# A graph-attention layer: the normalisation factor behind the row gather, a search moved from the loop into the drain, norms and transposes moved among TensorE's waits

## The chip, the cores and the metric

One core of a Trainium2 chip. The time is device microseconds of one execution, median of several; lower is better. A profile of one execution gives the spans and waits. The granted clock is the share of TensorE's full speed that the chip lets it run at; 1.00 is full speed. The core works with TensorE (PE), VectorE (DVE), ScalarE (ACT), GpSimd (POOL), SyncE (SP), and 16 DMA engines.

## The reference

```python
# x: 4096 x 512, adj: 4096 x 4096 (0, or up to 1e9), W: 512 x 2048, a: 4 heads x 1024
ht = (h @ W).reshape(N, 4, 512).transpose(1, 0, 2)
e = leaky_relu(src[:, :, None] + dst[:, None, :], 0.01) + adj[None]
att = softmax(e, axis=-1)
out = layernorm(x + einsum('hij,hjd->hid', att, ht).mean(axis=0))
```

The values of `adj` are so large that a row's softmax is nearly always 1 at its largest entry. The kernel therefore finds the largest entry of each row of `adj`, gathers that one row of `x`, multiplies it by the mean of the heads' weights, adds the row itself and normalises. A test (with norms as a bound) tells whether the second largest entry of any row comes near enough to matter; if so, a general path runs. It never runs on these inputs.

## The kernel before

4096 rows are 32 blocks of 128 (block 0 to 31). In step t of the loop VectorE reduces block t of `adj` to the maxima of 64 segments and finds the leading segment; GpSimd gathers that segment (`lead`, 64 numbers a row) from HBM; two steps later VectorE finds the place in it, and GpSimd gathers the row of `x` (`y`); a step later TensorE transposes it, ScalarE copies it out, TensorE multiplies it; ScalarE takes the statistics, and GpSimd makes of them the factor of normalisation (`rstd`). What follows the loop is called the drain. In the profile, MAX8 (`vector.max`) is the search for the eight largest entries of a row, and MATCH_VALUE_LOAD with FIND_INDEX8 (`max_index`) the search for their places.

```python
def find_segment(ib):
    seg = seg_of.pop(ib)
    nc.vector.max(out=top[:, ib, :], in_=seg)
    nc.vector.max_index(at, top[:, ib, :], seg)
    nc.gpsimd.tensor_tensor(row, at[:, 0:1], first[:, ib : ib + 1], op=OP.add)
    nc.gpsimd.indirect_dma_start(out=lead, in_=adj_segs, in_offset=...row...)
    ...
def find_inner(ib):
    nc.vector.max(out=inner[:, ib, :], in_=lead_of[ib])        # MAX8
def find_column(ib):
    find_inner(ib)
    nc.vector.max_index(within, inner[:, ib, :], lead_of.pop(ib))
    nc.gpsimd.tensor_tensor(col, at_of.pop(ib), within[:, 0:1], op=OP.add)
    gather_rows(ib, col)                                       # row gather: y
def finish_last(ib, residual):     # normalisation of one of the last four blocks, on VectorE
    ... tensor_add, bn_stats, bn_aggr ...
    nc.scalar.activation(r, mv[:, 1:2], AF.Sqrt, bias=eps)     # the root, on ScalarE
    nc.vector.reciprocal(r, r)
    nc.vector.tensor_scalar(hold[:, ib, :], o, mv[:, 0:1], r, ...)
# bound(0): largest norm, transposed by TensorE; bound(1): its root, broadcast by TensorE;
# bound(2): the bound itself on VectorE; test(): uses the bound, top and inner
# turn(ib): TensorE transposes y, ScalarE copies the result; products(ib, lo, hi): quarters lo to hi
```

In the profiles each engine takes its calls in program order: in the changed kernel ScalarE's copy for block 31 starts at 235.04 us, behind block 29's root at 234.84, and with the two calls swapped (a2_turn_first) at 230.71, ahead of the root at 234.13. So the place of a call among the others is its place in the engines' queues. All 32 stores are issued behind the loads (the last load at 200.92 us, the first store at 201.55); the last one, of block 31, waits for block 31's normalisation (its last part starts at 239.30, the store is issued at 240.14).

Of the kernel before, what the change touches and what calls it, by code (L numbers as in the profile page):

```python
# [9 lines left out]
F32 = mybir.dt.float32  # L10
# [9 lines left out]
P = 128  # L20
C = 512
E = 64
# [43 lines left out]
def leading_rows(ctx, tc, x, adj, W, a, out, ident, v, n_bad, any_bad):  # L66
# [7 lines left out]
    nc = tc.nc  # L74
    N, D = x.shape
    H = a.shape[0]
    KB, NB, S = D // P, N // P, N // E
    AHEAD = 5
    Q = 4
    PIECES = 4  # L80
    LATE = NB - Q
# [3 lines left out]
    small = ctx.enter_context(tc.tile_pool(name="small", bufs=5))  # L85
# [19 lines left out]
    def load_adj(ib):  # L105
        if 0 <= ib < NB:
            t = adj_t[ib] = adj_pool.tile([P, N], F32, name="adj_t")
            n = pieces(ib)
            for k in range(n):
                nc.sync.dma_start(t[:, ts(k, N // n)], adj_rows[ib][:, ts(k, N // n)])  # L110

    def load_x(lo, n):
        nc.sync.dma_start(hold[:, ds(lo, n), :], x_rows[:, ds(lo, n), :])
# [26 lines left out]
    top = once.tile([P, NB, 8], F32, name="top")  # L140
    inner = once.tile([P, NB, 8], F32, name="inner")
# [5 lines left out]
    seg_of, at_of, lead_of, y_t, yt_of, o_ps = {}, {}, {}, {}, {}, {}  # L147
# [12 lines left out]
# [3 lines that stand above are left out]
        at = small.tile([P, 8], U32, name="at")  # L163
        nc.vector.max_index(at, top[:, ib, :], seg)  # L164
        row = small.tile([P, 1], U32, name="row")
        nc.gpsimd.tensor_tensor(row, at[:, 0:1], first[:, ib : ib + 1], op=OP.add)  # L166
        lead = small.tile([P, E], F32, name="lead")
        nc.gpsimd.indirect_dma_start(  # L168
            out=lead, out_offset=None, in_=adj_segs,
            in_offset=bass.IndirectOffsetOnAxis(ap=row[:, :1], axis=0),  # L170
        )
        start = at_of[ib] = small.tile([P, 1], U32, name="start")
        nc.gpsimd.tensor_tensor(start, at[:, 0:1], width, op=OP.mult)  # L173
        lead_of[ib] = lead

    def gather_rows(ib, col):
        y = y_t[ib] = rows.tile([P, D], F32, name="y", bufs=4)
        nc.gpsimd.indirect_dma_start(  # L178
            out=y, out_offset=None, in_=x,
            in_offset=bass.IndirectOffsetOnAxis(ap=col[:, :1], axis=0),  # L180
        )

    def find_inner(ib):
        nc.vector.max(out=inner[:, ib, :], in_=lead_of[ib])

    def find_column(ib):
        find_inner(ib)
        within = small.tile([P, 8], U32, name="within")
        nc.vector.max_index(within, inner[:, ib, :], lead_of.pop(ib))  # L189
        col = small.tile([P, 1], U32, name="col")  # L190
        nc.gpsimd.tensor_tensor(col, at_of.pop(ib), within[:, 0:1], op=OP.add)  # L191
        gather_rows(ib, col)

    def find_column_in_row(ib):

        col = small.tile([P, 8], U32, name="col")
        nc.vector.max_index(col, top[:, ib, :], adj_t[ib])
        gather_rows(ib, col)

    def turn(ib):  # L200
        y = y_t.pop(ib)
        tp = psum.tile([P, KB, P], F32, name="tp", bufs=2)
        for kb in range(KB):
            nc.tensor.transpose(tp[:, kb, :], y[:, ts(kb, P)], ident)  # L204
        yt = yt_of[ib] = rows.tile([P, KB, P], F32, name="yt")
        nc.scalar.copy(yt, tp)  # L206
# [5 lines left out]
    def products(ib, lo=0, hi=KB):  # L212
        start = ib not in o_ps
        if start:
            o_ps[ib] = psum.tile([P, D], F32, name="o")
        for kb in range(lo, hi):
            nc.tensor.matmul(  # L217
                o_ps[ib], yt_of[ib][:, kb, :], w_sum[:, kb, :],
                start=(start and kb == 0), stop=(kb == KB - 1),
            )  # L220

    def row_norm(ib):
        sq = rows.tile([P, D], F32, name="sq")
        nc.scalar.activation(sq, hold[:, ib, :], AF.Square, accum_out=xx[:, ib : ib + 1])  # L224
# [8 lines left out]
    def rstd(i):  # L233
        nc.gpsimd.tensor_scalar(sd[:, i], sd[:, i], 1.0 / D, EPS, op0=OP.mult, op1=OP.add)  # L234
        nc.gpsimd.tensor_tensor(sd[:, i], sd[:, i], power[:, : i.stop - i.start], op=OP.pow)  # L235
        nc.gpsimd.tensor_mul(nm[:, i], nm[:, i], sd[:, i])  # L236
# [5 lines left out]
    def finish_last(ib, residual):  # L242

        o = o_ps.pop(ib)
        if residual:
            nc.vector.tensor_add(hold[:, ib, :], o, hold[:, ib, :])
            o = hold[:, ib, :]
        st = small.tile([P, nc.vector.BN_STATS_DIM], F32, name="st", bufs=2)
        nc.vector.bn_stats(st, o)
        mv = small.tile([P, nc.vector.BN_AGGR_DIM], F32, name="mv", bufs=2)  # L250
        nc.vector.bn_aggr(mv, st)
        r = small.tile([P, 1], F32, name="r", bufs=2)
        nc.scalar.activation(r, mv[:, 1:2], AF.Sqrt, bias=eps)
        nc.vector.reciprocal(r, r)
        nc.vector.tensor_scalar(hold[:, ib, :], o, mv[:, 0:1], r, op0=OP.subtract, op1=OP.mult)  # L255
# [52 lines left out]
    def bound(part):  # L308

        if part == 0:  # L310
            xm = once.tile([P, 1], F32, name="xm")
            nc.vector.tensor_reduce(xm, xx, axis=AX.X, op=OP.max)
            px = of_bound[0] = psum.tile([1, P], F32, name="px", bufs=1)
            nc.tensor.transpose(px, xm, ident)
        elif part == 1:
            nc.vector.tensor_reduce(xg, of_bound[0], axis=AX.X, op=OP.max)
            nc.scalar.activation(xg, xg, AF.Sqrt)
            pb = of_bound[1] = psum.tile([P, 1], F32, name="px", bufs=1)
            nc.tensor.matmul(pb, ones[0:1, :], xg, start=True, stop=True)
        else:  # L320
            nc.vector.tensor_mul(lead_by, of_bound[1], vn)
            nc.vector.tensor_scalar(lead_by, lead_by, 1.05, 110.0, op0=OP.mult, op1=OP.add)
# [3 lines left out]
    def test():  # L326
        a1 = top[:, :, 0]
        nc.vector.tensor_tensor(gap, top[:, :, 1], inner[:, :, 1], op=OP.max)
        size = once.tile([P, NB], F32, name="size")
        nc.vector.scalar_tensor_tensor(size, a1, -1.0, a1, op0=OP.mult, op1=OP.max)  # L330
        nc.vector.tensor_sub(gap, a1, gap)
        nc.vector.tensor_scalar(size, size, -(2.0 ** -22), lead_by, op0=OP.mult, op1=OP.subtract)
        nc.vector.scalar_tensor_tensor(gap, gap, 0.9999, size, op0=OP.mult, op1=OP.add)
        nc.vector.tensor_scalar(gap, gap, 0.0, None, op0=OP.is_gt)
# [18 lines left out]
    for t in range(NB):  # L353
        if t in x_at:
            load_x(*x_at[t])
        load_adj(t + AHEAD)
        middle = 1 if t == NB - 1 else 2
        segment_maxima(t, 0, middle)
        if t >= COLUMN:
            find_column(t - COLUMN)  # L360
        segment_maxima(t, middle, PIECES)
        find_segment(t)
        pair = t >= FINISH and t % 2 == 0
        if pair:
            rstd(slice(t - FINISH, t - FINISH + 2))
        if t < 2:
            mean_of_heads(t)
        elif t == 2:
            mean_of_heads(2)
            mean_of_heads(3)  # L370
        if t == 0:
            turn_a()
        turned = [(*vectors[0], turn_w(*vectors.pop(0))) for _ in range(vectors_at.get(t, 0))]
        if t == 16:
            head_norms()
        ib = t - PROJECT
        if ib >= 0:
            turn(ib)
            if ib < LATE:
                residual(ib)  # L380
        for some in turned:
            head_vector(*some)
        if ib >= 0:
            products(ib)
        if t >= STATS:
            stats(t - STATS)
            row_norm(t - STATS)
        if pair:
            finish(t - FINISH)
            finish(t - FINISH + 1)  # L390
# [4 lines left out]
    find_column(NB - 2)  # L395
    rstd(slice(NB - FINISH, NB - FINISH + 2))
    find_column_in_row(NB - 1)
    turn(NB - 3)
    products(NB - 3, 0, KB - 1)
    finish(NB - FINISH)  # L400
    finish(NB - FINISH + 1)
    for ib in range(LATE, NB):
        row_norm(ib)
    turn(NB - 2)
    products(NB - 3, KB - 1, KB)
    finish_last(NB - 4, True)
    find_inner(NB - 1)
    bound(0)
    products(NB - 2)
    bound(1)  # L410
    finish_last(NB - 3, True)
    bound(2)
    test()
    turn(NB - 1)
    for ib in (NB - FINISH, NB - FINISH + 1):
        store(nc.sync, ib, 1)
    residual(NB - 1)
# [244 lines left out]
```

## Time and profile before

| | before |
|---|---|
| time, median of the 4 runs beside the changed kernel | 248.11 us |
| span of the profiled run (247.19 us) | 245.3 us |
| busy: TensorE, VectorE, ScalarE, GpSimd | 82%, 77%, 45%, 40% |
| moved | 97.77 MB at 399 GB/s |
| end of the search through block 31's whole row (called F below) | 222.89 us |
| last store issued | 240.14 us |

A line of the order of time reads: start, duration, engine, line of the kernel, operation, output and input, shapes, how many were merged, and in brackets how long the engine had been idle and what released it. How the transfers and the drain look is shown in the prediction. Two more lines of VectorE, of block 30's tile, matter later:

```profile
204.71 2.27 DVE L155 TENSOR_REDUCE seg<-adj_t 128x32 f32<-128x2048 f32 x1
207.43 2.27 DVE L155 TENSOR_REDUCE seg<-adj_t 128x32 f32<-128x2048 f32 x1
```

Neither shows a wait. I read that as "the data had long been there". It had not: the packet records say that the last of the 16 engines delivered the first half at 204.66 and the second at 207.33, 0.05 and 0.10 us before VectorE took them.

### The profile page before, as it was taken

How to read it: one execution, taken by the hardware profiler on the slowest of the kernel's cores; microseconds unless marked ns; L12 is line 12 of the kernel's file. 1: busy time of each engine (PE TensorE's matmuls, PEld its weight loads, DVE VectorE, ACT ScalarE, POOL GpSimd, SP SyncE). 2: the span in 40 equal slices, each digit the busy share in tenths (PEclk: the TensorE clock that was granted, in tenths of full speed). 3: DMA queues.
4: the chain of work that ended last, by engine and by line, in shares of the span. 5: the costliest groups of instructions: out<-in, count | busy, mean ns of one | idle time of the engine just before them, and what ended most of it. 6: DMA issues, size and time to landing. Idle time of an engine off the chain costs nothing.

```text
span 245.3 us, 2538 instructions
## 1 busy us (share of the span) xinstructions
PE 200.4 (82%) x677; PEld 101.2 (41%) x678; DVE 188.7 (77%) x300; ACT 110.1 (45%) x266; POOL 97.6 (40%) x213
## 2 busy tenths in 40 slices
PE   0279948999999999999969777985969987987870
PEld 0135326555665555665334323332424432433320
DVE  2545686399689977998589979995998999966661
ACT  2012004044656565657645463744553846657110
POOL 1202423225616463646254535453455455652000
PEclk9999799599999999999999999999988999999995
DMA  7999999999999999999999999999999999999971
GB/s 257 435 428 414 422 423 425 418 424 408 425 416 415 415 414 422 422 402 431 418 418 413 426 412 421 408 424 416 416 414 390 412 408 400 409 401 376 402 294 55
DMA packets 16580, 97.77 MB, mean 399 GB/s; under 512 B 2472, under 2 KB 2472, under 8 KB 11184
## 3 DMA queue, kind: packets, MB, share of 16 engines
q1 hardware_dynamic: 12816, 87.82, 87.4%
q0 software_dynamic: 3584, 9.44, 10.0%
q10 hardware_dynamic: 160, 0.28, 0.3%
q8 instruction: 7, 0.11, 0.2%
q14 instruction: 13, 0.11, 0.1%
HBM read 89.15 MB, written 8.39 MB: 398 GB/s over the span
## 4 chain that ended last, share of the span: by engine, by line
DMA 35%; issue 26%; POOL 25%; DVE 7%; PE 4%; SPq 1%; POOLq 0%; ACT 0%; DVEq 0%
DMA adj_t<-in_adj_dram 29%; POOL y L178 8%; POOL lead L168 8%; DVE seg L155 5%; DMA lead<-in_adj_dram,row 3%; PE o L217 3%; DMA y<-in_x_dram,col 3%; POOL sd L235 3%; POOL row L166 2%; POOL start L173 2%; POOL col L191 1%; POOL sd L234 1%; POOL nm L236 1%; DVE hold L255 1%; SPq L110 1%
## 5 line engine op out<-in xcount | busy, mean ns | idle before, releaser
L155 DVE TENSOR_REDUCE seg<-adj_t 128x32 f32<-128x2048 f32 (+1 forms) x70 | 146.0, 2091 | 34.7 <-DMA adj_t<-in_adj_dram 34.5
L217 PE MATMUL o<-w_sum,yt 128*128 128x512 f32 x256 | 120.6, 613 | 1.3 <-ACT yt L206 1.3
L217 PEld LDWEIGHTS o<-w_sum,yt 128*128 128x128 f32 x256 | 47.1, 194 | 59.7 <-issue 47.0
L206 ACT COPY yt<-tp 128x512 f32<-128x512 f32 x32 | 18.8, 588 | 45.0 <-PE tp L204 44.9
L178 POOL DMA_INDIRECT y<-in_x_dram,col x32 | 32.2, 1008 | 16.7 <-POOL col L191 14.6
L168 POOL DMA_INDIRECT lead<-in_adj_dram,row x32 | 30.9, 964 | 15.5 <-POOL row L166 15.5
L204 PE MATMUL tp<-ident,y 128*128 128x128 f32 x128 | 19.7, 276 | 15.5 <-DMA y<-in_x_dram,col 15.3
L210 PE MATMUL o<-hold,ident 128*128 128x512 f32 x58 | 31.6, 627 | 0.8 <-DMA hold<-in_x_dram 0.8
L263 PE MATMUL o<-hold,ident 128*128 128x512 f32 x32 | 18.3, 724 | 15.7 <-DMA hold<-in_L_gnn_W_dram 15.7
L204 PEld LDWEIGHTS tp<-ident,y 128*128 128x128 f32 x128 | 14.4, 141 | 28.8 <-issue 27.4
L166 POOL TENSOR_TENSOR row<-at,first 128x1 uint32<-128x1 uint32 x32 | 5.9, 185 | 48.6 <-DVE at L164 47.4
L281 ACT COPY wt<-tp 128x512 f32<-128x512 f32 x16 | 9.2, 587 | 35.8 <-PE tp L279 35.8
L191 POOL TENSOR_TENSOR col<-start,within 128x1 uint32<-128x1 uint32 x31 | 5.9, 190 | 41.6 <-DVE within L189 41.6
L240 ACT ACTIVATE hold<-o,nm,sd 128x512 f32<-128x512 f32 x28 | 20.2, 771 | 2.5 <-POOL nm L236 2.5
L287 PEld LDWEIGHTS pv<-at_d,wt 128*128 128x128 f32 x128 | 17.2, 200 | 7.4 <-issue 3.9
L224 ACT ACTIVATE sq<-hold 128x512 f32<-128x512 f32 x32 | 19.8, 620 | 0.0
L231 ACT ACTIVATE sq<-o,nm 128x512 f32<-128x512 f32 x28 | 19.3, 688 | 0.9
L263 PEld LDWEIGHTS o<-hold,ident 128*128 128x128 f32 x32 | 7.2, 236 | 24.2 <-POOL row L166 10.4
L229 ACT ACTIVATE sq<-o 128x512 f32<-128x512 f32 x28 | 17.0, 607 | 0.0
L264 ACT ACTIVATE w_sum<-o 128x512 f32<-128x512 f32 x4 | 2.4, 598 | 31.7 <-PE o L263 31.7
L287 PE MATMUL pv<-at_d,wt 128*128 128x2 f32 x128 | 16.0, 249 | 0.6 <-ACT wt L281 0.6
L279 PEld LDWEIGHTS tp<-ident,hold 128*128 128x128 f32 x64 | 7.9, 142 | 6.9 <-issue 6.9
(73 smaller groups left out, 116.7 us busy)
## 6 DMA issues: line engine op xcount, KB each, us to landing
adj_t<-in_adj_dram SPq DMA_DIRECT2D x27, 2048.0 KB
out_dram<-hold SPq DMA_DIRECT2D x31, 256.0 KB
hold<-in_x_dram SPq DMA_DIRECT2D x7, 1024.0 KB
adj_t<-in_adj_dram SPq DMA_DIRECT2D x12, 512.0 KB
hold<-in_L_gnn_W_dram SPq DMA_DIRECT2D x4, 1024.0 KB
adj_t<-in_adj_dram SPq DMA_DIRECT2D x4, 1024.0 KB
hold<-in_x_dram SPq DMA_DIRECT2D x4, 256.0 KB
lead<-in_adj_dram,row POOLq DMA_INDIRECT x32, 5.8
```

The source lines that it names most:

```text
L155: nc.vector.tensor_reduce(seg_of[ib][:, ts(k, S // n)], adj_t[ib][:, ts(k, N // n)].rearrange("p (s e) -> p s e", e=E), axis=AX.X, op=OP.max,)
L168: nc.gpsimd.indirect_dma_start(out=lead, out_offset=None, in_=adj_segs, in_offset=bass.IndirectOffsetOnAxis(ap=row[:, :1], axis=0),)
L178: nc.gpsimd.indirect_dma_start(out=y, out_offset=None, in_=x, in_offset=bass.IndirectOffsetOnAxis(ap=col[:, :1], axis=0),)
L204: nc.tensor.transpose(tp[:, kb, :], y[:, ts(kb, P)], ident)
L206: nc.scalar.copy(yt, tp)
L210: nc.tensor.matmul(o_ps[ib], ident, hold[:, ib, :], start=True, stop=False)
L217: nc.tensor.matmul(o_ps[ib], yt_of[ib][:, kb, :], w_sum[:, kb, :], start=(start and kb == 0), stop=(kb == KB - 1),)
L224: nc.scalar.activation(sq, hold[:, ib, :], AF.Square, accum_out=xx[:, ib : ib + 1])
L231: nc.scalar.activation(sq, o, AF.Square, bias=nm[:, i], accum_out=sd[:, i])
L240: nc.scalar.activation(hold[:, ib, :], o_ps.pop(ib), AF.Identity, bias=nm[:, i], scale=sd[:, i])
L263: nc.tensor.matmul(o, ident, hold[:, w_at + kb * H + h, :], start=(h == 0), stop=(h == H - 1))
L287: nc.tensor.matmul(pv[:, kb, h : 2 * H : H], wt[:, k, :], at_d[:, k, h : 2 * H : H], start=(k == 0), stop=(k == KB - 1),)
```

## The change

Its intent: get VectorE through the last blocks sooner by taking a MAX8 out of each (the search can use `top`, which holds the same largest value; the second largest in the segment is needed only by the test at the end), let the row gather go ahead of the factor on GpSimd, and fill TensorE's waits in the drain.

```diff
-        lead = small.tile([P, E], F32, name="lead")
+        lead = small.tile([P, E], F32, name="lead", bufs=2 * Q + 1)
...
     def find_column(ib):
-        find_inner(ib)
+        if ib < LATE - Q:                     # LATE - Q is 24
+            find_inner(ib)
-        nc.vector.max_index(within, inner[:, ib, :], lead_of.pop(ib))
+        nc.vector.max_index(within, top[:, ib, :], lead_of[ib])
...
-        find_segment(t)
         pair = t >= FINISH and t % 2 == 0
         if pair:
             rstd(slice(t - FINISH, t - FINISH + 2))
+        find_segment(t)
...                                            # the drain
     find_column_in_row(NB - 1)
+    for ib in range(LATE, NB):
+        row_norm(ib)
     turn(NB - 3)
+    bound(0)
     products(NB - 3, 0, KB - 1)
     finish(NB - FINISH)
     finish(NB - FINISH + 1)
-    for ib in range(LATE, NB):
-        row_norm(ib)
     turn(NB - 2)
     products(NB - 3, KB - 1, KB)
+    bound(1)
+    bound(2)
     finish_last(NB - 4, True)
-    find_inner(NB - 1)
-    bound(0)
-    products(NB - 2)
-    bound(1)
+    for ib in range(LATE - Q, NB):
+        find_inner(ib)
+    test()
+    products(NB - 2, 0, KB - 1)
     finish_last(NB - 3, True)
-    bound(2)
-    test()
     turn(NB - 1)
+    products(NB - 2, KB - 1, KB)
```

## The prediction

> **What bounds the kernel now.** I read the page first, then stretches of the last 45 us, then the chain of waits, then the order of time on VectorE and GpSimd before the drain. The page's slices of 6.13 us say that the transfers set the pace almost to the end:

> ```profile
> DMA  7999999999999999999999999999999999999971
> GB/s 257 435 428 414 422 423 425 418 424 408 425 416 415 415 414 422 422 402 431 418 418 413 426 412 421 408 424 416 416 414 390 412 408 400 409 401 376 402 294 55
> ```

> Both rows are flat through slice 38. 97.77 MB go through; at the 415 GB/s of the middle that alone is 236 us of the 245.3 us span. Nothing in the change removes a byte, so only the last two slices are open to it. The stretches of 2 us show where the full load ends:

> ```profile
> 234.00:236.00 2.00, 2.00 (x6) 0.80 (x5) 1.53 (x5) 0.29 (x1) 0.00 (x0) 1.00 1.05 402
> 236.00:238.00 2.00, 1.79 (x6) 0.38 (x4) 1.07 (x5) 0.00 (x0) 0.00 (x0) 1.00 0.74 283
> 238.00:240.00 2.00, 0.00 (x0) 0.00 (x0) 1.57 (x4) 0.29 (x1) 0.00 (x0) 1.00 0.08 25
> 240.00:242.00 2.00, 0.00 (x0) 0.00 (x0) 0.11 (x1) 0.00 (x0) 0.00 (x0) 0.54 0.36 131
> ```

> The last two columns are DMA share and GB/s. Output stores fill the engines until about 237.5; then they stand idle until the last store, issued at 240.14, of row block 31. So the arithmetic that leads to the last store trails the transfers by some 2.6 us, and that is all a shorter drain can win: even a perfect one leaves about 245.8 of 248.46 us. The chain of waits over the drain (start, us, what):

> ```profile
> 219.21 6.63 DMA y<-in_x_dram,col
> ...
> 228.74 3.44 PE o L217 x8
> 232.17 0.31 PE px L319 x2
> 232.48 0.59 PE tp L204 x4
> 233.07 0.86 PE o L210 x2
> 233.93 2.66 PE o L217 x6
> 236.58 0.15 PE px L338 x2
> 236.73 1.07 PE o L217 x2
> ...
> 239.30 0.81 DVE hold L255
> ```

> A row gather of 6.63 us, then TensorE nearly back to back, then the last normalisation on VectorE. Ahead of it, one row block on VectorE:

> ```profile
> 201.33 0.22 DVE L184 MAX8 inner<-lead 128x8 f32<-128x64 f32 x1
> 201.65 0.09 DVE L189 MATCH_VALUE_LOAD within<-inner,lead 128x8 f32 x1
> 201.73 0.22 DVE L189 FIND_INDEX8 within<-inner,lead 128x8 uint32<-128x64 f32 x1
> 201.86 2.27 DVE L155 TENSOR_REDUCE seg<-adj_t 128x32 f32<-128x2048 f32 x1
> ```

> From 188.7 to 215.9 VectorE never waits for a transfer: it trails the matrix, block after block, in steps of 5.56 us. The MAX8 takes the place of 0.32 us (201.33 to 201.65): 0.22 busy, 0.10 until the search that reads its result. And GpSimd puts the normalisation factor (L234 to L236) between two gathers:

> ```profile
> 212.40 0.19 POOL L234 TENSOR_SCALAR sd<-sd 128x2 f32<-128x2 f32 x1
> 212.68 0.72 POOL L235 TENSOR_TENSOR sd<-sd,power 128x2 f32<-128x2 f32 x1
> 213.48 0.20 POOL L236 TENSOR_TENSOR nm<-nm,sd 128x2 f32<-128x2 f32 x1
> 213.63 0.19 POOL L191 TENSOR_TENSOR col<-start,within 128x1 uint32<-128x1 uint32 x1
> ```

> The index search for that column (`within`) was over at 212.01, so 1.6 us of the gather's delay is the factor.

> [...] here the instruction shows 0.96 us and the chain 6.63 us, so I count gathers from issue to landing.[...]

> **The change, part by part.** The order of instructions was compared with the one before.

> 1. *MAX8 of `lead` leaves the loop for blocks 24 to 31.* The search uses `top`, whose first entry is the same value. Six leave the loop; the one in block 26's step is swallowed by the 0.83 us wait for data at 187.05. Five are worth 5 x 0.32 = 1.6 us: the loop on VectorE ends at about 214.3 instead of 215.9. Packets counted up in the trace put the last piece of the matrix at 211.7, where VectorE begins it at 214.2 now and would at 212.6: late enough.

> 2. *Factor before the segment's row, after the row gather* (on even steps). Block 29's row gather, issued at 214.21, loses both the 1.6 us of factor ahead of it and most of VectorE's 1.6: some 2.4 us earlier. In return block 30's segment gather, issued at 211.14, is now behind the factor (0.19 + 0.72 + 0.20 and gaps, 1.2 us): from a VectorE shift of 1.3 it keeps about 1.2, so 209.9. It landed 5.8 us after issue by the packets (211.14 to 216.95), so 215.7 now, and VectorE, ready at 214.3, waits 1.4 us for it, as it waits 1.42 us now.

> 3. *Search of block 30's column and of block 31's full row.* From landing to the end of the search in 64 elements it is 218.40 - 216.95 = 1.45 now; without the MAX8 in between about 0.95. With 4.5 us for the search through 4096 (4.42 and its value load) the searches end at F = 220.5 instead of 222.89: 2.35 us earlier. Both last row gathers go that much earlier.

> 4. *The drain after F.* Norms (four squares of 0.62 us) come ahead of a copy on ScalarE, and end at about 220.3, just under F. On TensorE the bound's transposition waits for F (+0.5), three quarters of block 29's products follow (2.84), the transposition of block 30 (F + 3.2, its row then being there), the last quarter, and the bound's broadcast at F + 4.6. VectorE stands idle from F + 0.8 until then; now it does block 28's normalisation in that time. After the broadcast VectorE has, in order: bound 0.7, block 28's normalisation 2.65 (228.98 to 231.63 for the same five now), eight MAX8 at about 0.14 apart and one latency 1.3, test 0.95, and 1.65 of block 29 until its root. That root stands on ScalarE ahead of the copy that the last products need. Root 0.3, copy to first product 0.64, products, count and last quarter 4.07 (233.76 to 237.83), last statistics to store 2.31 (237.83 to 240.14). Sum: F + 4.6 + 0.7 + 2.65 + 1.3 + 0.95 + 1.65 + 0.3 + 0.64 + 4.07 + 2.31 = F + 19.2.

> Now it is 240.14 - 222.89 = F + 17.25. So the drain starts 2.35 us earlier and is 1.9 us longer, and the store goes out at 239.7 instead of 240.14. I predict a gain of about 0.5 us: 248.0 us.

> **Rivals.** (a) *TensorE sets the drain's end*: if VectorE does its share faster, products for block 31 would follow those of block 30 without a pause, at about F + 11, and the store go out 2.5 to 3 us earlier: 245.8, the transfers' floor above. For it: TensorE's own work does shrink in pauses, as intended. Against: the root of block 29 is issued ahead of the last copy. (b) *No head start*: if block 30's segment gather lands no earlier, because its 5.8 us stretch under load or the factor holds it, F stays at 222.3 or so and the longer drain shows: store at 241.5, 249.8 us.[...] (c) *The transfers decide*: stores now run at full load until 237.5 whatever VectorE does; then a store at 238 or 240 costs only itself. It caps (a), and makes the loop's part worth nothing by itself.

> **Range and chances.** Runs of before spread over 1.26 us, some 0.5% of the time. With the shift of F unsure by 1 us and VectorE's stretch by 1, I take 246.2 to 249.4. Two per cent is 5 us: faster by that would need bytes saved (0.03); slower by that needs a wait nobody planned (0.02).

> **What would show it.** Right: no MAX8 in VectorE's last six steps and eight together near 230; the loop's last segment search ending about 214.3; block 31's full-row search ending about 220.5; VectorE idle some 4 us behind it, until the bound's broadcast; TensorE idle before the last block's products, released by ScalarE's copy, and that by the root; the transfers' full load ending at 237.5 still. Wrong: TensorE without that pause and a store before 238 (rival a), or a full-row search that ends after 222 (rival b). If the slices in the middle gain or lose GB/s, everything here is beside the point.

## The result, and the profile after

The changed kernel took 250.77 us in the median (250.05 to 250.99, 4 runs), the kernel before 248.11 (247.33 to 249.02, 4 runs). Ratio 1.0101, 95% interval 1.0058 to 1.0144: slower by about 1%, clearly not a gain, and outside the stated range. A ratio here is the mean time of one kernel's runs over that of the other's of the same rounds, so not quite the ratio of the medians. Executions over 1.5% slower than the fastest of the same kernel are left out of the means.

The page's transfers, in 40 slices (now of 6.22 us):

```profile
DMA  7999999999999999999999999999999999999921
GB/s 253 413 424 420 424 428 419 415 425 405 421 419 414 420 406 431 416 412 425 411 422 416 418 420 420 405 422 416 414 408 399 410 405 399 409 395 395 391 94 54
```

The middle is as before: no bytes were won or lost. Slice 39 fell from 294 to 94 GB/s: the stores were done, and the core waited longer for its last one. It was issued at 243.76 instead of 240.14, 3.62 us later. That splits into two parts.

**The loop did not get shorter.** VectorE at block 30, in order of time:

```profile
205.55 2.29 DVE L155 TENSOR_REDUCE seg<-adj_t 128x32 f32<-128x2048 f32 x1 [1.18 <-DMA adj_t<-in_adj_dram]
207.75 0.08 DVE L191 MATCH_VALUE_LOAD within<-top,lead 128x8 f32 x1
207.82 0.22 DVE L191 FIND_INDEX8 within<-top,lead 128x8 uint32<-128x64 f32 x1
208.40 2.29 DVE L155 TENSOR_REDUCE seg<-adj_t 128x32 f32<-128x2048 f32 x1 [0.36 <-DMA adj_t<-in_adj_dram]
```

The MAX8 is gone from between the reductions, as planned. But VectorE now waits 1.18 and 0.36 us for the two halves of the tile: 1.54 us, the 1.6 us that the five MAX8 were to save. The last reduction of the loop ends at 216.03 (before: 215.38), block 30's segment gather is issued at 212.13 (before: 211.14), and F is 223.52 instead of 222.89: 0.63 us later, not 2.35 earlier. Of these, 0.44 us were there already at the first reduction of block 27, which waits for its data in both kernels and starts at 188.32 instead of 187.88.

**The drain got longer**, from F + 17.25 to F + 20.24. Its chain in order of time:

```profile
228.15 0.16 DVE L323 TENSOR_TENSOR lead_by<-px,vn 128x1 f32<-128x1 f32 x1 [3.90 <-PE px L321]
...
231.06 1.10 DVE L184 MAX8 inner<-lead 128x8 f32<-128x64 f32 x8
...
234.84 0.29 ACT L255 ACTIVATE r<-mv,eps 128x1 f32<-128x1 f32 x1 [4.47 <-DVE mv L253]
235.04 0.57 ACT L208 COPY yt<-tp 128x512 f32<-128x512 f32 x1
...
235.66 4.54 PE L219 MATMUL o<-w_sum,yt 128*128 128x512 f32 x6 [2.62 <-ACT yt L208]
```

VectorE stands idle for 3.90 us until the bound is broadcast, then does block 28's normalisation, eight MAX8, the test and the start of block 29's normalisation, before the root (L255) can go. Only behind that root stands the copy that block 31's products need, and TensorE has waited 2.62 us for it. All of this was foreseen. What was not is the 4.54 us. The same six pieces in the kernel before:

```profile
233.76 2.82 PE L217 MATMUL o<-w_sum,yt 128*128 128x512 f32 x6
```

The stretches of 2 us (length, then busy time with count of TensorE, its weight loads, VectorE, ScalarE, GpSimd, then TensorE's granted clock, DMA share, GB/s) say why:

```profile
232.00:234.00 2.00, 1.04 (x3) 0.19 (x1) 1.86 (x10) 0.00 (x0) 0.00 (x0) 1.00 1.05 404
234.00:236.00 2.00, 0.34 (x1) 0.34 (x2) 1.57 (x5) 0.77 (x2) 0.00 (x0) 0.95 1.04 399
236.00:238.00 2.00, 2.00 (x3) 0.73 (x3) 1.55 (x4) 0.29 (x1) 0.00 (x0) 0.50 0.55 209
238.00:240.00 2.00, 2.00 (x4) 0.58 (x2) 0.55 (x1) 0.00 (x0) 0.00 (x0) 0.70 0.30 112
```

After the pause the granted clock is 0.50. The clock records have it at half from 235.81 for 3.413 us, beginning right as the products start (235.66). Before, it was 1.00 from 185.53 to 240.14. In both profiles the clock changes only at whole multiples of 3.413 us from one another: this fall comes 75.1 us after the end of the one before (160.71), 22 times 3.413. Such a stretch of 3.413 us, counted from the changes of the same profile, is called a window below. In the window before this fall, from 232.39, TensorE had 0.80 us of products; the last section comes back to that.

### The profile page after: what moved, and what is told of

The parts are those of the page before. It is cut to its first block, busy times and chain, and to the rows that moved or that the text cites.

```text
span 248.9 us, 2520 instructions
## 1 busy us (share of the span) xinstructions
PE 203.3 (82%) x677; PEld 102.4 (41%) x678; DVE 186.3 (75%) x300; ACT 109.4 (44%) x266; POOL 97.3 (39%) x213
## 2 busy tenths in 40 slices
DMA packets 16581, 97.77 MB, mean 393 GB/s; under 512 B 2473, under 2 KB 2473, under 8 KB 11185
## 4 chain that ended last, share of the span: by engine, by line
DMA 44%; PE 23%; issue 10%; DVE 10%; POOL 8%; ACT 2%; SPq 0%; POOLq 0%; DVEq 0%
DMA adj_t<-in_adj_dram 20%; DMA hold<-in_x_dram 13%; PE o L219 12%; DMA hold<-in_L_gnn_W_dram 11%; DVE seg L155 4%; PE o L265 3%; PE pv L289 3%; POOL lead L168 2%; POOL y L178 2%; PE o L212 2%; DVE col L199 2%; PE tp L281 1%; PE tp L206 1%; POOL sd L237 1%; DVE st L251 1%
## 5 line engine op out<-in xcount | busy, mean ns | idle before, releaser
L155 DVE TENSOR_REDUCE seg<-adj_t 128x32 f32<-128x2048 f32 (+1 forms) x70 | 146.2, 2094 | 41.2 <-DMA adj_t<-in_adj_dram 40.7
L178 POOL DMA_INDIRECT y<-in_x_dram,col x32 | 30.8, 963 | 17.8 <-POOL col L193 15.7
L168 POOL DMA_INDIRECT lead<-in_adj_dram,row x32 | 32.2, 1007 | 13.9 <-POOL row L166 13.9
L265 PE MATMUL o<-hold,ident 128*128 128x512 f32 x32 | 22.1, 856 | 16.3 <-DMA hold<-in_L_gnn_W_dram 16.3
L212 PE MATMUL o<-hold,ident 128*128 128x512 f32 x58 | 31.4, 624 | 0.0
L233 ACT ACTIVATE sq<-o,nm 128x512 f32<-128x512 f32 x28 | 19.2, 687 | 0.9
L265 PEld LDWEIGHTS o<-hold,ident 128*128 128x128 f32 x32 | 8.4, 275 | 27.1 <-POOL row L166 11.7
L289 PEld LDWEIGHTS pv<-at_d,wt 128*128 128x128 f32 x128 | 16.3, 191 | 6.8 <-ACT wt L283 3.7
L289 PE MATMUL pv<-at_d,wt 128*128 128x2 f32 x128 | 15.3, 244 | 0.6 <-ACT wt L283 0.6
```

Source lines behind the costliest of these rows:

```text
L155: nc.vector.tensor_reduce(seg_of[ib][:, ts(k, S // n)], adj_t[ib][:, ts(k, N // n)].rearrange("p (s e) -> p s e", e=E), axis=AX.X, op=OP.max,)
L168: nc.gpsimd.indirect_dma_start(out=lead, out_offset=None, in_=adj_segs, in_offset=bass.IndirectOffsetOnAxis(ap=row[:, :1], axis=0),)
L178: nc.gpsimd.indirect_dma_start(out=y, out_offset=None, in_=x, in_offset=bass.IndirectOffsetOnAxis(ap=col[:, :1], axis=0),)
L212: nc.tensor.matmul(o_ps[ib], ident, hold[:, ib, :], start=True, stop=False)
L233: nc.scalar.activation(sq, o, AF.Square, bias=nm[:, i], accum_out=sd[:, i])
L265: nc.tensor.matmul(o, ident, hold[:, w_at + kb * H + h, :], start=(h == 0), stop=(h == H - 1))
```

## The experiments

Theory 1: the loop's moves are worth nothing, because the transfers hold VectorE; the drain loses by its order (root before copy, more work in VectorE's chain) and by the pauses, with TensorE's clock at half behind them (0.50 for 3.413 us in the profile above). Rivals: the clock is by the way; the moves in the loop lose, not the drain; VectorE's chain or late gathers set the end whatever the order. Each kernel ran beside the kernel before on the same chip. All gave correct results.

| run | median us | before | ratio (95%) | F | last store | F to store |
|---|---|---|---|---|---|---|
| kernel before, first profile | 248.11 | | | 222.89 | 240.14 | 17.25 |
| changed, first profile | 250.77 | 248.11 | 1.0101 (1.0058 to 1.0144) | 223.52 | 243.76 | 20.24 |
| a8_changed_again | 250.69 | 247.51 | 1.0151 (1.0103 to 1.0199) | 223.06 | 243.28 | 20.22 |
| a1_fill | 249.16 | 247.52 | 1.0065 (1.0018 to 1.0112) | 222.99 | 241.56 | 18.57 |
| a9_two_fills | 249.10 | 247.78 | 1.0046 (1.0024 to 1.0068) | 223.69 | 242.22 | 18.53 |
| a2_turn_first | 247.86 | 247.52 | 1.0004 (0.9967 to 1.0042) | 222.82 | 240.45 | 17.63 |
| a3_drain_only | 248.13 | 247.52 | 1.0028 (0.9981 to 1.0075) | 222.56 | 240.66 | 18.10 |
| a4_factor_only | 247.46 | 247.51 | 1.0017 (0.9976 to 1.0057) | 222.85 | 239.93 | 17.08 |
| a5_defer_only | 246.76 | 247.51 | 0.9980 (0.9938 to 1.0022) | 222.53 | 241.66 | 19.13 |
| a6_reordered | 247.19 | 247.52 | 0.9977 (0.9930 to 1.0024) | 223.03 | 239.99 | 16.96 |
| a7_old_loop_new_drain | 246.77 | 247.51 | 0.9967 (0.9933 to 1.0001) | 222.93 | 239.67 | 16.74 |
| a10_mended_filled | 246.03 | 247.78 | 0.9938 (0.9914 to 0.9962) | 222.95 | 238.84 | 15.89 |

F and the last store are of the profiled execution, one per kernel; the times are of six executions, in the first two rows of four.

### a1_fill: work for TensorE in the second pause

```diff
+    idle = psum.tile([P, D], F32, name="o")
+    for _ in range(3):
+        nc.tensor.matmul(idle, ident, hold[:, NB - 1, :], start=True, stop=True)
     residual(NB - 1)
```

> The changed kernel with three products of the identity (their sum thrown away) put into TensorE's pause of 2.62 us before block 31's products. Theory 1 (the pause halves TensorE's granted clock, and that costs 1.7 us after it): the clock stays at 1.0 in the drain, the six halves of products take 2.84 us instead of 4.54, the last store goes out 1.7 us earlier, about 249.1 us. Theory 2 (the products are slow for another reason, such as loads on the memory or missing records): products still near 4.5 us, 250.8 us. If the extra products themselves delay block 31's residual by more than the pause, the start of its products moves past the copy.

The clock stayed at 1.0 in the drain, and the six pieces of product, still behind the same root and copy, were back to their length:

```profile
235.16 2.84 PE L219 MATMUL o<-w_sum,yt 128*128 128x512 f32 x6
```

F to last store fell by 1.67 us, the median came out at 249.16 against the expected 249.1. In the profile three products that nobody reads bring the drain's products back to full speed: theory 1's clock is shown, its rival is out. In time this run alone isn't clear of the changed kernel's first comparison (the intervals 1.0018 to 1.0112 and 1.0058 to 1.0144 overlap); a9_two_fills against a8_changed_again is.

### a2_turn_first: the copy before the root

```diff
     products(NB - 2, 0, KB - 1)
-    finish_last(NB - 3, True)
     turn(NB - 1)
+    finish_last(NB - 3, True)
```

> The changed kernel with block 31's transposition and copy put before block 29's normalisation in the program, so ScalarE copies before it takes the root. Theory 1 (the order of the root and the copy on ScalarE makes TensorE wait, and the pause halves the clock): TensorE without the pause, copy right behind the transposition (about 231.3), then VectorE's chain of three normalisations is the end: last store about 2.5 us earlier than 243.76, 248.3 us. Rival (VectorE's chain sets the end anyhow, the copy is only in its shadow): less than 1 us gained, 250 us or more.

ScalarE copied right behind the transposition, TensorE had no pause there (block 31's products start at 232.17; the two before them start at 231.32 and take 1.02 us), and the last store came 3.3 us earlier than in the changed kernel's first profile (2.6 of it between F and the store). The end is now VectorE's chain, three normalisations one behind the other:

```profile
230.71 0.59 ACT L208 COPY yt<-tp 128x512 f32<-128x512 f32 x1 [1.04 <-PE tp L206]
...
238.15 0.68 DVE L251 BATCH_NORM_STATS2 st<-o 128x6 f32<-128x512 f32 x1
```

The last statistics start as soon as VectorE is through with what stands before them, 2 us after the products. The swap of two lines undoes nearly all of the loss: 1.0004.

### a3_drain_only: the old loop with the changed drain

```diff
         (in words: the loop as in the kernel before; the drain as in the changed kernel, but)
-    for ib in range(LATE - Q, NB):
-        find_inner(ib)
+    find_inner(NB - 1)
```

> The kernel before in its loop (factor and MAX8 where they were), the changed drain (with one MAX8 instead of eight in it). Theory 1 (the drain's order is the loss, the loop's two moves are worth nothing because the transfers hold VectorE): as slow as the changed kernel less seven MAX8 at 0.14 us, about 249.8 us. Rival (the loop's moves are what loses, the drain gains as intended): 247.5 us or less.

248.13 us: slower by 0.3%, with an interval that includes no change, and not by the expected 0.9%. The expectation took half the clock for granted. With one MAX8 in the chain instead of eight the root came earlier, TensorE's pause was 1.74 us instead of 2.62, and the clock did not fall in it (the six pieces behind it took 2.84 us). 249.8 less the 1.7 us of clock is 248.1. So the drain's order without the seven extra MAX8 costs little (F to last store 0.85 us longer than before); most of the rest comes with the pause and the half clock after it.

### a8_changed_again: the changed kernel once more

> The changed kernel itself, once more and beside the next three. Theory 1: the drain's last products again behind a TensorE pause of about 2.6 us; whether the clock halves there depends on where the pause falls, so the single times may split by up to 1.7 us. Median 249.5 to 250.8 us, ratio about 1.008. If it comes out within 0.3% of the kernel before, the loss of the first comparison was chance.

1.0151: the loss is no chance. The profile has a turn that I had not expected. The second pause (2.62 us) was there again, at full clock: the products after it took 2.84 us. Instead the clock had fallen at the first pause, where TensorE waited for block 28's row:

```profile
212.00:214.00 2.00, 1.36 (x4) 0.29 (x2) 2.00 (x5) 0.95 (x2) 1.69 (x4) 1.00 1.04 411
214.00:216.00 2.00, 0.00 (x0) 0.00 (x0) 1.91 (x3) 0.00 (x0) 0.45 (x1) 0.89 0.98 390
216.00:218.00 2.00, 1.27 (x5) 0.90 (x6) 0.30 (x2) 0.82 (x2) 1.06 (x2) 0.50 1.07 409
218.00:220.00 2.00, 2.00 (x3) 0.96 (x4) 1.70 (x4) 1.97 (x7) 1.07 (x4) 0.50 1.04 408
220.00:222.00 2.00, 2.00 (x3) 0.68 (x3) 2.00 (x1) 2.00 (x7) 1.47 (x4) 0.50 1.05 403
```

Half clock from 215.58 for two windows (6.827 us). Block 28's products took 5.96 us instead of 3.70, which pushed block 29's transposition to 223.62 (220.84 in the first profile) and with it the broadcast (5.9 us behind F instead of 4.2). F to last store is 20.22 us by this way and 20.24 by the other. A pause of 2.62 us before block 31's products was followed by half clock in one run and by full clock in the other. Where it lay differed. In the first profile it fell into one window whole (232.39 to 235.81), and TensorE had 0.80 us of products in that window; here the edge of two windows (236.06) cut it, and the first of them, from 232.65, had 1.62 us of products (see the last section).

### a9_two_fills: work in both pauses

```diff
+        if t == NB - 1:
+            busy = psum.tile([P, D], F32, name="o")
+            for _ in range(2):
+                nc.tensor.matmul(busy, ident, w_sum[:, 0, :], start=True, stop=True)
         if ib >= 0:
             turn(ib)
... and the three products of a1_fill
```

> The changed kernel with idle products in both of TensorE's pauses: two ahead of block 28's transposition, three ahead of block 31's products. Theory 1[...]: the clock stays at 1.0 from 185 us to the end of the products, searches to last store F + 18.6, median 248.6 to 249.0 us, against 250.7 for the changed kernel. What is left over the kernel before, some 1.2 us, is then the drain's order (root before copy, eight MAX8 in the chain). Rival (the clock is by the way): 250 us or more, as the changed kernel.

The clock was at 1.0 from 185.62 to 243.64, and block 28's eight products took 3.70 us (5.96 in a8_changed_again). F to last store was 18.53 (expected 18.6), median 249.10 (0.1 us over what was expected), and the six times lie within 1.4 us (a1_fill's, with one pause filled, within 3.2). The interval is clear of a8_changed_again's. What is left, 0.5%, goes with the drain's order and its eight MAX8: F to last store is 1.28 us longer than before.

### a4_factor_only: only the factor moved

```diff
-        find_segment(t)
         pair = ...
         if pair:
             rstd(slice(t - FINISH, t - FINISH + 2))
+        find_segment(t)
```

> The kernel before with the factor alone moved ahead of the segment's search. Theory A[...]: block 27's row gather issued at about 202.2 instead of 203.09, the second half of block 30's tile complete at about 208 instead of 207.3, VectorE waits for it, the searches end no earlier than in the kernel before (222.9, within 0.4): 247.5 to 248.2 us. Rival (taking the factor out of the gather's way is a gain): block 30's and 31's row gathers earlier by 1 us, 246.8 us.

Time and F are about as theory A has them (247.46, 222.85), but not in the way it expected: block 27's gather did not move (203.05), and VectorE shows no wait for block 30's tile (it starts on the second half 0.10 us after its last part, 207.77 after 207.67). Block 29's gather did go out 1.0 us earlier (213.19 instead of 214.21), the way the prediction said (it had 2.4 us from both moves), and it is worth nothing: block 30's and 31's gathers (219.16, 223.61), which the end hangs on, stand where they stood.

### a5_defer_only: only the MAX8 deferred

```diff
         (lead with 9 buffers, search on top, MAX8 in the loop only below block 24, as in the change)
     find_column_in_row(NB - 1)
+    for ib in range(LATE - Q, NB - 1):
+        find_inner(ib)
     turn(NB - 3)
```

> The kernel before with the MAX8 of blocks 24 to 30 alone deferred into VectorE's idle 1.3 us behind the full-row search. Theory A (the transfers hold VectorE's loop, so time taken off VectorE turns into waiting for the next tile): new waits of 1 to 1.6 us in all for block 30's and 31's tiles, loop end no more than 0.4 us earlier than 215.4: 247.3 to 247.9 us. The prediction's step (five MAX8 at 0.32 us bring the loop's end and all behind it 1.6 us forward): loop end at 213.8, 246.2 us.

The direct test of the prediction's first step. VectorE at block 30:

```profile
205.29 2.29 DVE L155 TENSOR_REDUCE seg<-adj_t 128x32 f32<-128x2048 f32 x1 [1.21 <-DMA adj_t<-in_adj_dram]
```

The saved time is waited away at this tile; the loop's last reduction ends at 215.42, against 215.38 before and 213.8 by the prediction. The 0.36 us by which F is earlier comes from the MAX8 no longer standing between block 30's segment and its search. The median, 246.76, is lower than theory A said, though its interval includes no change at all. The six times are 246.4 to 246.8 four times, and 248.6 and 248.8. The profiled one is a slow one of these: clock at half for 3.4 us from 218.74, after a pause of 2.55 us before block 28's transposition; block 28's eight products took 5.40 us instead of 3.70. That the other slow one has the same cause is likely, but no profile shows it.

### a6_reordered and a7_old_loop_new_drain: the drain mended

```diff
     finish(NB - FINISH + 1)
+    finish_last(NB - 4, True)
     turn(NB - 2)
     products(NB - 3, KB - 1, KB)
     bound(1)
-    bound(2)
-    finish_last(NB - 4, True)
     for ib in range(LATE - Q, NB):
         find_inner(ib)
+    bound(2)
     test()
     products(NB - 2, 0, KB - 1)
-    finish_last(NB - 3, True)
     turn(NB - 1)
+    finish_last(NB - 3, True)
```

> The changed kernel with the drain's order mended: block 28's normalisation and the eight MAX8 go into VectorE's idle stretch before the bound's broadcast, and block 31's copy stands before block 29's root. Theory 1: broadcast, test and normalisation of 29 and 30 follow without a gap, TensorE has no pause over 1 us and keeps its clock, last store about 239.4 if the searches end at 223.5 as they did, about 246.5 us: 0.6% under the kernel before. Rival (transfers or the late gathers decide): no better than the kernel before, 248 us.

> The kernel before in its loop, with the mended drain of the reordered kernel (one MAX8 instead of eight). Theory 1: searches end at 222.6 to 222.9, last store about F + 16, 238.8, TensorE without a pause over 1 us, clock at 1.0 until the last products: 246.5 us, 0.4% under the kernel before. Rival (nothing in the drain's order beyond the copy matters): as the reordered kernel, within 0.1%.

Block 28's normalisation and the eight MAX8 went into VectorE's idle stretch, the copy before the root. With the changed loop (a6) that gives 247.19 us, with the old one (a7, one MAX8) 246.77; neither is clear of the kernel before. Both stores came 0.6 to 0.9 us later than expected, and both profiles have the clock at half early in the drain (218.10 and 217.59, 3.413 us each; the mean granted clock is 0.57 from 218 to 222 in a6 and 0.50 from 218 to 220 in a7), after a pause before block 28. In a6 TensorE was busy for 0.66 us of the 4 from 214 to 218. In a7 that pause was 1.64 us:

```profile
216.43 0.63 PE L204 MATMUL tp<-ident,y 128*128 128x128 f32 x4 [1.64 <-DMA y<-in_x_dram,col]
217.74 5.31 PE L217 MATMUL o<-w_sum,yt 128*128 128x512 f32 x8 [0.68 <-ACT yt L206]
```

### a10_mended_filled: a7 with one idle product

```diff
+        if t == NB - 1:
+            busy = psum.tile([P, D], F32, name="o")
+            nc.tensor.matmul(busy, ident, w_sum[:, 0, :], start=True, stop=True)
         if ib >= 0:
             turn(ib)
```

> The kernel before in its loop, mended drain, and one idle product in the pause of 1.5 us ahead of block 28's transposition, where the clock halved at 217.6. Theory 1: clock at 1.0 there, block 28's products end 1 us or more earlier, last store about 238.8: 246.2 us, 0.5% under the kernel before. Rival (late gathers hold the drain, so the clock there costs nothing): 246.8 us, as without the filler.

Clock 1.0 up to 239.34 (1.00 in every stretch of 2 us from 216 to 222 and from 234 to 238), and block 28's products at their proper length:

```profile
218.09 3.70 PE L217 MATMUL o<-w_sum,yt 128*128 128x512 f32 x8 [0.67 <-ACT yt L206]
```

Last store at 238.84 (expected 238.8), 246.03 us (expected 246.2), 0.62% under the kernel before with an interval clear of it. Its median is the lowest, though its interval overlaps with a7's (0.9933 to 1.0001); what the one product does is read from the profile. The kernel is the loop of the kernel before with the mended drain and one product that nobody reads.

## Why the prediction was wrong

- **The bound.** "Only the last two slices are open to it" was right: the stores kept the transfers full until about 236 in the profiles looked at there (DMA share 1.05 from 234 to 236 in the kernel before and in a10_mended_filled, 1.04 in the changed kernel), and the differences lie in when the last store goes out.
- **Step 1 failed**, in its last sentence: "Packets counted up in the trace put the last piece of the matrix at 211.7 ... late enough." It looked at the wrong tile and at the wrong moment. Wrong tile: block 30's halves came before block 31's pieces and were already short. Wrong moment: counted bytes give the landing of the mean; in the profiles VectorE takes a half behind the last of the 16 engines (at 207.43 behind 207.33 in the kernel before, at 208.40 behind 208.37 in the changed one). That undoes the sentence for block 31 too: in the kernel before, the last engine delivered its last piece at 213.44, not 211.7, so VectorE could not have begun it at 212.6. In the changed kernel the increments for the second half of block 30 arrive from 205.47 to 208.37. That the kernel before showed no wait at block 30 meant only that VectorE arrived 0.05 and 0.10 us behind the data. Five times 0.32 us became 1.18 + 0.36 us of waiting; a5_defer_only shows the same for this part alone.
- **Step 2** was half right. Block 29's row gather could go earlier (1.0 us in a4_factor_only). But the factor's move was not worth anything there, and block 30's segment gather, expected at 209.9, left at 212.13: not because of the factor (it was done at 211.15, before the segment was known) but because VectorE found the segment later, behind the waits of step 1. With both moves block 30's tile also lands later. Counted from the first reduction of block 27, so that what came earlier drops out, its second half was complete after 20.05 to 20.26 us (changed kernel: 188.32 to 208.37) in the six profiles with both moves, after 19.50 (a4) and 19.67 (a5) with one, and after 19.45 to 19.48 (kernel before: 187.88 to 207.33) in the four with the old loop. So both moves together put the tile back by 0.6 to 0.8 us; whether the earlier gathers do it is open.
- **Step 3** was right as a step: 0.5 us were to be saved between the landing of block 30's segment and F, and 0.63 were (5.94 us before, 218.21 to 223.52 = 5.31 after). Its sum has a slip: 215.7 + 0.95 + 4.5 is 221.15, not 220.5. With that, F comes 1.74 us earlier instead of 2.35, the store at 240.35 (221.15 + 19.2), and the forecast gain of 0.5 us is a loss of 0.2: the prediction's own terms did not carry a gain. The step also started from a landing 2.5 us later than the predicted 215.7.
- **Step 4** had the mechanism right and one term mis-sized. Bound's broadcast 4.21 us behind F (predicted 4.6), bound 0.68 (0.7), block 28 2.65 (2.65), MAX8 1.14 (1.3), test 0.97 (0.95), to the root 1.67 (1.65), root to copy 0.20 (0.3), copy to product 0.62 (0.64), last part 2.32 (2.31). But products, count and last quarter took 5.78 instead of 4.07. I wrote that TensorE would stand "idle before the last block's products", and did not ask what its clock would be behind the pause; it was 0.50, and that was the 1.71 us. All in all F + 20.24 for F + 19.2.
- **The rivals.** (b), "no head start", is what happened to F, with 249.8 us for it. The profiled store (243.76) went out 2.26 us behind (b)'s 241.5: F was 1.22 us later than (b)'s 222.3, and the drain 1.04 us longer than F + 19.2, which is the clock's 1.71 less 0.67 for terms smaller than foreseen. (a) was rightly put aside: the root did hold the copy.
- **The sum.** F later by 0.63, drain longer by 2.99 (1.71 of it clock, 1.28 order): 3.62 us at the last store of the profiled run; the two profiled executions took 250.9 and 247.19 us. The medians of that comparison differ by 2.7; the profiled execution of the kernel before was faster than all four timed ones. The profiles differ in whether, where and for how long the clock falls; that the unprofiled executions differ for the same reason is likely, but not shown.

## What to carry to other kernels

An engine without a recorded wait may still start only just behind its data (0.05 and 0.10 us at block 30 in the kernel before): before counting on time taken off it, compare its start with the arrival of the last part of each tile that it will now reach sooner. In a drain, look at what stands in front of a copy on another engine's queue: in the changed kernel block 29's root held the copy for block 31, and TensorE waited 2.62 us for it. And a pause on TensorE can be paid twice, once as the pause and once as half a clock after it: so it was here behind pauses of 2.62, 2.70 and 1.64 us, and not behind others of 1.74 and 2.62 us, with more products in the window. Cheap products in the pause bought that back in a1_fill (1.67 us between F and the last store) and in a10_mended_filled (0.85 us).
